# Four attention, scan and convolution layers over eight images: the scans' second product moved from GpSimd to VectorE, key sums taken as four pair sums on TensorE, and three evacuations moved to ScalarE

## The chip, the cores and the metric

The kernel runs on one core of a Trainium2 chip. The core has five engines that run at the same time, each in the order of its own instruction list, and wait for one another by semaphores: TensorE (PE, with its weight loads as PEld), VectorE (DVE), ScalarE (ACT), GpSimd (POOL) and SyncE (SP), which here issues transfers only. The metric is device time in microseconds, from one launch for all eight images. Three runs of the kernel before took 5807.06, 5814.95 and 5815.47 us; their median, 5814.95 us, is the time before.

## The reference

The input is eight images of 256 channels and 32 x 32 pixels, in float32. Four layers follow one another, the first three each as `x + layer(group_norm(x))`:

```python
x = x + _L0_conv_ref(_gn(x), w_qkv, w_out, b_out)   # attention, 8 heads of 64, q and k normalised
x = x + _L1_conv_ref(_gn(x), scaling, quant_w, bias) # 3x3 convolution, 256 -> 256, weights +-1
x = x + _L2_conv_ref(_gn(x), kernel, bias)           # 3x3 convolution, 256 -> 256
x = x + _L3_conv_ref(_gn(x), ...)                    # scans, gates, mixer attention, projections
```

Layer 0 normalises q and k of a head along the 1024 pixels, forms `sim = q k * 10` (1024 x 1024 per head), takes the softmax over the keys and multiplies with v. In layer 3 the 256 channels are cut into four branches of 64. Each branch is widened to 128 channels and passes a selective scan with 16 states per channel, step by step over the 1024 pixels:

```python
h = exp(dt * A) * h + (dt * u) * B     # per channel, state and pixel
y = sum over states of h * C           # + u * D afterwards
```

After the scans come a gate, depthwise convolutions over the pixels, a second attention with 8 heads of 32 (called the mixer here), a Gelu, a depthwise 3x3 convolution and a last projection.

## The kernel before

All work is float32. An image occupies two tiles of 128 channels x 1024 pixels. The stages of an image are recorded as streams, each named by a letter: A (layer 0: q, k, v, attention), O (its output projection), C (the two convolutions), N (norms ahead of the scans), F0 to F3 (what a branch needs before its scan), S (the scans of the four branches), Z0 to Z3 (what follows a branch's scan), B (gates, depthwise convolutions, mixer attention) and E (the end of the image).

**The order is planned on the host.** The engines' methods are wrapped, so that the code records operations instead of issuing them (`Plan`, `Recorded`). `arrange` then lays down an order for all engines together: `gather` joins matmuls into groups, `depend` finds which group needs which and which tiles of rotating pools it uses, `appraise` gives each group a duration from a formula (`cost`, and `STAGGER` for matmuls on parts of the array), and `rank` gives each a due time. The due times come from the table `PACE`: four marks for each stream and image, and a group's due time lies between them by its place in the stream. `arrange` repeatedly takes the engine that can begin earliest and gives it the ready group that can begin soonest, and of equals the one with the earlier due time. A tile of a pool is handed out in the order of due times, and a group that needs a tile waits until one is free. `issue` then emits the instructions in this order, and since every one passes through one helper, all of them carry one line number in the profile, L251. Only the tiles' names tell them apart. The planner's durations decide the order alone, not the time on the chip.

**Attention of layer 0** (`attention`, from L1166, and `pair` in `front_attention`). Two heads make a pair, so an image has four pairs; queries go in two halves of 512 and keys in eight tiles of 128. For each of the 64 steps of an image, two matmuls put scores of 128 keys x 512 queries for both heads into a PSUM tile `big`, ScalarE takes the exponential into a work tile `p` (128 x 1024), and two matmuls multiply `p` with the values into `acc`. VectorE adds the eight `p` of a half into the first of them, with seven `tensor_add` (L1210). After the eighth, `take` sums that tile over its 128 partitions by two matmuls with a matrix of ones, 128 x 64, one per head. The sums go to DRAM, are read back as a 128 x 16 tile `few`, inverted, and spread (`invert`, L1139).

**q, k and v.** `q_and_k` (L1240) copies the projected q and k out of PSUM by VectorE (`a<-big`, shown as `q<-big` and `k<-big`), after which ScalarE squares the PSUM tile for the norms. The four value tiles of an image are copied by VectorE too (L1348). In the mixer, q and k leave PSUM by VectorE with their bias (L1797 to L1802).

**The scans** (`scan_steps`, from L1610). A unit is one branch, one half of the pixels, four states and two of the four groups of 32 channels: 16 units a branch, 64 an image, 512 in all. Its steps are:

```python
pool.tensor_mul(u["hs"], u["du"], both_groups(u["bc"][:, 0]))        # drive: (dt u) B
scalar.activation(u["da"], u["dt"][:, e], AF.Exp, scale=a_neg[...])  # decay, twice, into PSUM
vector.tensor_tensor_scan(hs[:, e], u["da"], hs[:, e], ...)          # scan, twice
pool.tensor_mul(hs, hs, both_groups(u["bc"][:, 1]))                  # weigh: h C
```

In the first half of the pixels, GpSimd also copies the last column of the states (`carry`) for the second half. Every two units, four matmuls with `sel` (128 x 32 each, on the four column parts of the array) add the states into the PSUM tile `y`. The tile `da` has one buffer, `hs` has five. `dt`, `dt u`, B and C of a branch travel through DRAM (`dt_m`, `du_m`, `bc`) to be spread over the partitions; their DRAM pool `dp` has two buffers, and the pool `xdp` that holds the images between C and N has five.

Of the kernel before, what the change touches and what calls it, by code (L numbers as in the profile page):

```python
# [12 lines left out]
F32 = mybir.dt.float32  # L13
# [7 lines left out]
P = 128  # L21
# [13 lines left out]
STAGGER = {(128, 128): 5, (64, 128): 109, (128, 64): 56, (128, 32): 29, (32, 128): 300}  # L35
# [3 lines left out]
        (-805, -722, -708, -698),  # L39
        (-23, 574, 666, 1155),  # L40
        (1968, 2114, 2121, 2171),
        (2852, 2904, 2935, 2987),
        (3583, 3699, 3701, 3730),
        (4216, 4274, 4274, 4274),
        (4659, 4763, 4763, 4927),
        (5576, 5668, 5690, 5902),
    ),
    "B": (
        (2421, 2445, 2644, 2827),
        (3198, 3198, 3283, 3439),  # L50
        (4035, 4035, 4118, 4140),
        (4510, 4598, 4600, 4614),
        (4974, 5354, 5544, 5568),
        (7158, 7158, 7256, 7330),
        (7367, 7615, 7789, 8025),
        (9252, 9434, 9574, 9654),
    ),
    "C": (
        (686, 764, 875, 875),
        (1836, 1987, 2190, 2310),  # L60
        (2369, 2615, 2813, 2937),
        (3296, 3424, 3555, 3745),
        (3992, 4153, 4243, 4479),
        (4472, 4553, 4705, 5147),
        (5548, 5760, 5769, 5918),
        (6309, 6309, 6610, 6714),
    ),
    "E": (
        (2851, 2914, 2949, 3105),
        (3537, 3696, 3801, 3995),  # L70
        (4164, 4309, 4454, 4659),
        (4641, 4925, 5037, 5526),
        (5491, 5660, 5966, 6452),
        (7236, 7974, 8650, 9020),
        (7803, 9469, 9931, 11379),
        (12457, 12492, 12572, 12586),
    ),
    "F0": (
        (291, 291, 349, 383),
        (-602, -270, 49, 2139),  # L80
        (-2209, -2209, -2137, -2137),
        (246, 246, 425, 454),
        (-8960, -8951, -8951, -8832),
        (-1537, -1537, -1537, -1537),
        (-184, -33, 0, 66),
        (4973, 5375, 5378, 5378),
    ),
    "F1": (
        (-437, -436, 487, 491),
        (1752, 1794, 2099, 2171),  # L90
        (49, 129, 515, 3272),
        (3649, 3649, 3706, 3756),
        (4505, 4544, 4594, 4660),
        (2018, 2580, 2690, 2690),
        (5341, 5341, 5353, 5389),
        (4210, 4210, 4210, 4264),
    ),
    "F2": (
        (959, 1013, 1013, 1013),
        (2528, 2641, 2641, 2741),  # L100
        (2573, 3389, 3391, 3447),
        (3918, 4165, 4242, 4261),
        (4191, 4357, 4693, 4693),
        (5559, 5574, 5631, 5782),
        (335, 364, 364, 558),
        (6297, 6519, 6549, 6549),
    ),
    "F3": (
        (1911, 1946, 1948, 1989),
        (2794, 2817, 2817, 2817),  # L110
        (3441, 3441, 3499, 3656),
        (4222, 4328, 4338, 4341),
        (4837, 4862, 4988, 4988),
        (5691, 5860, 5899, 5903),
        (3559, 3559, 3559, 3559),
        (-9601, -9073, -8842, -8730),
    ),
    "N": (
        (-1664, -1664, -1401, -1293),
        (-687, -686, -686, -684),  # L120
        (2795, 3121, 3168, 3219),
        (3804, 3804, 3899, 4110),
        (-242, -22, 1040, 1289),
        (3745, 3749, 3758, 3792),
        (2961, 6267, 6777, 6846),
        (7316, 7506, 7510, 8044),
    ),
    "O": (
        (-582, -391, -354, -341),
        (1469, 1485, 1612, 1612),  # L130
        (2194, 2342, 2343, 2362),
        (3043, 3147, 3181, 3227),
        (3823, 3844, 3951, 4031),
        (4410, 4410, 4410, 4420),
        (5280, 5286, 5297, 5414),
        (6015, 6195, 6218, 6218),
    ),
    "S": (
        (-1634, -1316, -1316, -1316),
        (2298, 2626, 2633, 2722),  # L140
        (3026, 3409, 3755, 3809),
        (3937, 3937, 3937, 3937),
        (516, 2314, 2400, 3371),
        (4794, 4794, 4794, 4846),
        (-550, -490, -490, -490),
        (7436, 7512, 7560, 7593),
    ),
    "V": (
        (463, 463, 764, 872),
    ),  # L150
    "Z0": (
        (-600, -478, -313, -275),
        (-3647, -3176, -3168, -3168),
        (-1138, -1134, -1134, -1132),
        (4211, 4217, 4407, 4407),
        (4725, 4725, 4816, 4915),
        (5804, 5873, 6100, 6457),
        (6544, 6544, 6573, 6597),
        (5426, 5431, 5448, 5490),
    ),  # L160
    "Z1": (
        (-192, 110, 744, 744),
        (2693, 2704, 2773, 2908),
        (2239, 2427, 2448, 2456),
        (4041, 4041, 4551, 4558),
        (4595, 4620, 4620, 4752),
        (5520, 5591, 5873, 5886),
        (1357, 1455, 1455, 1910),
        (2656, 2851, 2916, 3215),
    ),  # L170
    "Z2": (
        (1072, 1232, 1232, 1232),
        (2983, 2983, 2983, 2991),
        (3547, 3551, 3551, 3769),
        (4325, 4372, 4389, 4397),
        (4751, 4773, 4936, 5085),
        (5992, 6074, 6084, 6129),
        (6864, 7140, 7211, 7360),
        (8225, 8272, 8329, 8329),
    ),  # L180
# [2107 lines left out]
```

## Time and profile before

| | |
|---|---|
| Median of three runs | 5814.95 us (5807.06 to 5815.47) |
| Profiled execution | 5817.3 us, span 5815.6 us |
| Mean granted TensorE clock | 0.896 |
| PE busy | 4872.9 us (84%) |
| DVE busy | 3930.9 us (68%) |
| ACT busy | 2709.1 us (47%) |
| POOL busy | 2611.0 us (45%) |
| 512 drives on POOL | 1248.5 us, 2446 ns each |
| 512 weighs on POOL | 1289.2 us, 2519 ns each |
| 448 additions of `p` on DVE | 601.2 us, 1343 ns each |

Times in the profile are microseconds unless marked ns, from one execution. A matmul of 512 float32 columns appears as two records. The chain of waits is followed back from the last instruction, and at each step to what released it; its shares say what set the end. A group's row gives the count, the busy time, the mean of one, and the idle time of its engine just before it with what ended that. A row of a stretch gives the length, then the busy time of PE, PEld, DVE, ACT and POOL with their instruction counts, then the granted TensorE clock as a share of full speed, and the DMA share and rate.

### The profile page before, as it was taken

The page shows a single profiled execution, that of the slowest core. Times are in us where ns is not written, and L with a number is a line of the kernel's source. Part 1 is how long each engine was busy: PE and PEld are TensorE (multiplying, and loading weights), DVE is VectorE, ACT ScalarE, POOL GpSimd, SP SyncE. Part 2 cuts the span into 40 slices and gives each one's busy share as a digit, 9 for nine tenths or more (in the row PEclk, how much of TensorE's full clock was granted, in tenths as well). Part 3 has the DMA queues.
Part 4 walks back from the last instruction along what each step waited for, and adds up shares of the span by engine and source line. Part 5 has one row for each costly group of instructions (what it writes and reads, how often), then busy time and mean ns, then how long its engine had stood idle before and what let it go on. Part 6 is the DMA issues. An engine that isn't in the chain of part 4 may idle for free.

```text
span 5815.6 us, 55053 instructions
## 1 busy us (share of the span) xinstructions
PE 4872.9 (84%) x18086; PEld 1946.9 (33%) x18086; DVE 3930.9 (68%) x5060; ACT 2709.1 (47%) x3353; POOL 2611.0 (45%) x1295
## 2 busy tenths in 40 slices
PE   8998678778998879979899889888899767787695
PEld 3345323322423144332434323332335521221223
DVE  5545787767876667776787657775797775567723
ACT  3333344455453644446354554446453335556342
POOL 0000766287502854046560745518343378287600
PEclk9999889888998889989899989989999877888796
DMA  3123434244413343133522433224333544233301
GB/s 115 42 59 111 120 93 129 73 126 125 110 39 96 104 131 99 53 106 99 145 71 73 138 98 101 82 71 115 99 93 116 146 114 115 62 97 101 88 19 36
DMA packets 262409, 553.34 MB, mean 95 GB/s; under 512 B 65880, under 2 KB 89048, under 8 KB 262112
## 3 DMA queue, kind: packets, MB, share of 16 engines
q1 hardware_dynamic: 178016, 413.36, 25.3%
q10 hardware_dynamic: 84096, 136.35, 8.2%
q8 instruction: 146, 2.39, 0.2%
q14 instruction: 151, 1.24, 0.1%
HBM read 478.72 MB, written 62.39 MB: 93 GB/s over the span
## 4 chain that ended last, share of the span: by engine, by line
PE 49%; DVE 19%; DMA 10%; ACT 8%; POOL 7%; issue 5%; SPq 1%; ACTq 0%; DVEq 0%; POOLq 0%
PE big L251 27%; PE acc L251 9%; PE cv L251 9%; POOL hs L251 7%; DVE hs L251 6%; ACT p L251 3%; DMA dt_m<-dt 2%; ACT da L251 2%; PE y L251 2%; DMA dt<-dt_m 2%; DVE p L251 2%; SPq L251 1%; DVE u L251 1%; DVE room L251 1%; DMA du<-du_m 1%
## 5 line engine op out<-in xcount | busy, mean ns | idle before, releaser
L251 POOL TENSOR_TENSOR hs<-du,bc 128x1024 f32<-128x1024 f32 x512 | 1248.5, 2446 | 2408.6 <-DMA du<-du_m 2157.4
L251 POOL TENSOR_TENSOR hs<-hs,bc 128x1024 f32<-128x1024 f32 x512 | 1289.2, 2519 | 297.7 <-DVE hs L251 251.0
L251 ACT ACTIVATE p<-big 128x1024 f32<-128x1024 f32 x1024 | 1018.4, 1019 | 670.0 <-PE big L251 582.5
L251 ACT ACTIVATE da<-dt,a_neg 128x512 f32<-128x512 f32 x1024 | 707.8, 691 | 1207.1 <-DVE hs L251 956.5
L251 PE MATMUL acc<-p,v 128*64 128x512 f32 x3072 | 854.1, 640 | 141.5 <-ACT p L251 133.3
L251 DVE TENSOR_TENSOR_SCAN hs<-da,carry,hs 128x512 f32<-128x512 f32 x512 | 654.7, 1279 | 333.9 <-ACT da L251 293.8
L251 PE MATMUL cv<-taps,w 128*128 128x256 f32 x3072 | 762.6, 402 | 105.3 <-DVE taps L251 35.4
L251 DVE TENSOR_TENSOR_SCAN hs<-da,hs 128x512 f32<-128x512 f32 x512 | 623.7, 1218 | 330.0 <-ACT da L251 241.5
L251 PEld LDWEIGHTS cv<-taps,w 128*128 128x128 f32 x3072 | 597.7, 200 | 346.8 <-issue 136.6
L251 DVE TENSOR_TENSOR p<-p 128x1024 f32<-128x1024 f32 x448 | 601.2, 1343 | 163.0 <-ACT p L251 125.0
L251 PE MATMUL big<-q,k 64*128 64x512 f32 x2048 | 597.3, 667 | 57.3 <-ACT p L251 33.0
L251 PE MATMUL y<-hs,sel 128*32 128x512 f32 x2048 | 413.3, 689 | 206.4 <-POOL hs L251 199.2
L251 PEld LDWEIGHTS acc<-p,v 128*64 128x64 f32 x3072 | 164.9, 139 | 744.3 <-issue 373.3
L251 PE MATMUL big<-qk,qk 32*128 32x512 f32 x2048 | 369.1, 697 | 46.2 <-ACT raw L251 14.0
L251 PEld LDWEIGHTS big<-q,k 64*128 64x128 f32 x2048 | 164.7, 193 | 448.1 <-issue 236.1
L251 PE MATMUL cv<-p,v 128*64 128x512 f32 x1024 | 288.1, 636 | 2.7 <-DVE xt L251 2.7
L251 PE MATMUL big<-xn,w 128*128 128x512 f32 x512 | 233.5, 606 | 4.3 <-DVE v L251 3.4
L251 PEld LDWEIGHTS y<-hs,sel 128*32 128x32 f32 x2048 | 57.2, 114 | 497.5 <-POOL hs L251 364.7
L251 PEld LDWEIGHTS big<-qk,qk 32*128 32x128 f32 x2048 | 101.9, 198 | 299.8 <-issue 196.4
L251 PE MATMUL big<-o,w 128*128 128x512 f32 x384 | 189.8, 640 | 11.3 <-issue 5.7
L251 POOL COPY carry<-hs 128x2 f32<-128x2 f32 x256 | 107.4, 420 | 169.1 <-DVE hs L251 145.6
L251 DVE SCALAR_TENSOR_TENSOR u<-raw,vec,u 128x1024 f32<-128x1024 f32 x96 | 142.6, 1485 | 37.4 <-ACT u L251 36.4
(228 smaller groups left out, 5448.8 us busy)
## 6 DMA issues: line engine op xcount, KB each, us to landing
bc<-bc SPq DMA_DIRECT2D x1024, 128.0 KB
w<-wc ACTq DMA_DIRECT2D x384, 256.0 KB
dt<-dt_m SPq DMA_DIRECT2D x512, 128.0 KB
du<-du_m SPq DMA_DIRECT2D x512, 128.0 KB
rs<-inv SPq DMA_DIRECT2D x64, 256.0 KB
dt_m<-dt SPq DMA_DIRECT2D x64, 256.0 KB
du_m<-a SPq DMA_DIRECT2D x64, 256.0 KB
w<-in_wqk ACTq DMA_DIRECT2D x64, 128.0 KB
```

What stands on the lines that cost most here:

```text
L251: made = op["call"](*args, **kwargs).ins
```

## The change

- The weigh is a product on VectorE, and the carry copy is one on ScalarE.
- VectorE adds each second `p` to the one before it. This leaves four sums of two per half instead of one sum of eight. `take` sums all four over the partitions: eight matmuls with ones of 128 x 32, even pair sums into rows 0 and 32 and odd ones into rows 64 and 96, which leaves two partial sums for each head. One transfer carries the four rows to DRAM instead of two; `invert` reads two `few` and adds them on VectorE.
- The copies of q, k and v in layer 0, and q and k of the mixer with their bias, are ScalarE's. (The value tile of the mixer stays with VectorE.)
- In the planner: a fill (a transfer from DRAM or a memset into a pool tile) is due no earlier than its first use; a matmul group also claims the tile `v` or `x` that its evacuation will write; the assumed extra time of matmuls on 32 rows is 90 instead of 300; every mark in `PACE` is new. In the kernel before, the marks of S begin at -1634, 2298, 3026, 3937, 516, ...; in the new table they begin at 496, 980, 1470, 1967, 2458, 2907, 3371, 3655.
- `dp` has four buffers and `xdp` eight.

```diff
-STAGGER = {(128, 128): 5, (64, 128): 109, (128, 64): 56, (128, 32): 29, (32, 128): 300}
+STAGGER = {(128, 128): 5, (64, 128): 109, (128, 64): 56, (128, 32): 29, (32, 128): 90}
+CLAIMED = (("vp", "v"), ("xp", "x"))
...
+    users = defaultdict(list)
+    for n, op in enumerate(ops):
+        for a in op["ins"]:
+            if in_psum(a):
+                users[a.tensor.name].append(groups[of[n]])
+    for g in groups:
+        if g.engine == 0:
+            out = ops[g.ops[0]]["outs"][0].tensor.name
+            for u in users[out]:
+                for t in u.tiles:
+                    if rooms[t][0] in CLAIMED and t not in g.tiles:
+                        g.tiles.append(t)
...
+    first_use = [None] * len(groups)
+    for n in reversed(range(len(groups))):
+        if groups[n].fetches and first_use[n] is not None:
+            due[n] = max(due[n], first_use[n])
+        for k in groups[n].after:
+            first_use[k] = due[n] if first_use[k] is None else min(due[n], first_use[k])
...
-    dp = plan.pool("dp", 2, space=DRAM)
+    dp = plan.pool("dp", 4, space=DRAM)
...
-    xdp = plan.pool("xdp", 5, space=DRAM)
+    xdp = plan.pool("xdp", 8, space=DRAM)
...
-            if add_up:
-                if kt == 0:
-                    pair["sum"] = u["p"]
-                else:
-                    vector.tensor_add(pair["sum"], pair["sum"], u["p"])
+            if kt == 0:
+                pair["sums"] = []
+            if kt % 2 == 0:
+                pair["sums"].append(u["p"])
+            else:
+                total = pair["sums"][-1]
+                vector.tensor_add(total, total, u["p"])
...
-                vector.tensor_copy(a, ps)
+                scalar.copy(a, ps)
                 scalar.activation(ps, ps, AF.Square, accum_out=ss[:, i : i + 1])
...
+                for n, total in enumerate(totals):
+                    for e in range(2):
+                        at = (2 * (n % 2) + e) * 32
+                        tensor.matmul(
+                            ps[at : at + 32, 0:HALF],
+                            ones,
+                            total[:, HALVES[e]],
+                            start=n < 2,
+                            stop=n >= len(totals) - 2,
+                        )
...
-            vector.tensor_copy(
-                v[:, kt : kt + 2].rearrange("p a b -> p (a b)"), ps
-            )
+            scalar.copy(v[:, kt : kt + 2].rearrange("p a b -> p (a b)"), ps)
...
-                pool.tensor_copy(carry[:, u["q"], g : g + 2], hs[:, :, HALF - 1])
-            pool.tensor_mul(hs, hs, both_groups(u["bc"][:, 1]))
+                scalar.copy(carry[:, u["q"], g : g + 2], hs[:, :, HALF - 1])
+            vector.tensor_mul(hs, hs, both_groups(u["bc"][:, 1]))
...
-                    vector.tensor_scalar(
-                        q, ps, col("ain_b", t), 32.0**-0.5, ALU.add, ALU.mult
+                    scalar.activation(
+                        q, ps, AF.Identity, bias=q_b[:, t : t + 1], scale=32.0**-0.5
                     )
...
-                    vector.tensor_scalar_add(k, ps, col("ain_b", at))
+                    scalar.activation(k, ps, AF.Identity, bias=col("ain_b", at))
```

## The prediction

> **What bounds the kernel now.** I read the page's busy shares first, then the chain of waits, then the scan's groups, then the stretches between the first and last state sum of each image.
>
> ```profile
> PE 4872.9 (84%) x18086; PEld 1946.9 (33%) x18086; DVE 3930.9 (68%) x5060; ACT 2709.1 (47%) x3353; POOL 2611.0 (45%) x1295
> ...
> PE 49%; DVE 19%; DMA 10%; ACT 8%; POOL 7%; issue 5%; SPq 1%; ACTq 0%; DVEq 0%; POOLq 0%
> PE big L251 27%; PE acc L251 9%; PE cv L251 9%; POOL hs L251 7%; DVE hs L251 6%; ACT p L251 3%; DMA dt_m<-dt 2%; ACT da L251 2%; PE y L251 2%; DMA dt<-dt_m 2%; DVE p L251 2%; SPq L251 1%; DVE u L251 1%; DVE room L251 1%; DMA du<-du_m 1%
> ```
>
> TensorE is the fullest engine, yet only half of the chain is its own. The other half is latency, largely of the scans: POOL `hs`, DVE `hs`, ACT `da`, and the transfers of `dt` and `du`.
>
> ```profile
> 625.00:1062.00 437.00, 330.92 (x1149) 117.37 (x1148) 353.15 (x356) 195.35 (x259) 317.04 (x150) 0.86 0.40 111
> 1184.00:1596.00 412.00, 346.72 (x1402) 137.35 (x1398) 310.44 (x321) 210.31 (x280) 305.27 (x152) 0.89 0.44 122
> 3917.00:4460.00 543.00, 486.29 (x1961) 184.44 (x1960) 400.13 (x500) 290.82 (x373) 309.85 (x152) 0.96 0.39 107
> 4614.00:4975.00 361.00, 243.68 (x888) 82.66 (x878) 240.91 (x207) 157.60 (x204) 295.68 (x147) 0.78 0.42 115
> 5097.00:5488.00 391.00, 292.19 (x1088) 93.30 (x1084) 293.58 (x272) 196.41 (x241) 315.73 (x153) 0.82 0.37 105
> ```
>
> These rows are the scans of images 0, 1, 5, 6 and 7. POOL has the same 300 us or so of work in each: 57% of image 5's stretch, but 73% to 82% of the others. There POOL sets the pace, and TensorE works at low density (busy time times granted clock, over the length): 0.65, 0.75, 0.86, 0.53 and 0.61. Over the whole span, fine stretches added up the same way give 4432 us of full-clock work, a density of 0.76.
>
> ```profile
> L251 POOL TENSOR_TENSOR hs<-du,bc 128x1024 f32<-128x1024 f32 x512 | 1248.5, 2446 | 2408.6 <-DMA du<-du_m 2157.4
> L251 POOL TENSOR_TENSOR hs<-hs,bc 128x1024 f32<-128x1024 f32 x512 | 1289.2, 2519 | 297.7 <-DVE hs L251 251.0
> ...
> L251 DVE TENSOR_TENSOR p<-p 128x1024 f32<-128x1024 f32 x448 | 601.2, 1343 | 163.0 <-ACT p L251 125.0
> ```
>
> ```profile
> 2617.80 1.28 DVE L251 TENSOR_TENSOR_SCAN hs<-da,carry,hs 128x512 f32<-128x512 f32 x1 [0.76 <-ACT da L251]
> ...
> 2619.12 0.69 ACT L251 ACTIVATE da<-dt,a_neg 128x512 f32<-128x512 f32 x1
> ...
> 2619.91 1.28 DVE L251 TENSOR_TENSOR_SCAN hs<-da,carry,hs 128x512 f32<-128x512 f32 x1 [0.83 <-ACT da L251]
> ...
> 2621.96 1.28 DVE L251 TENSOR_TENSOR_SCAN hs<-da,carry,hs 128x512 f32<-128x512 f32 x1 [0.76 <-ACT da L251]
> ```
>
> With one `da` buffer, decay and scan alternate: scans start 2.1 us apart, 4.2 us a unit. POOL needs 2.45 + 2.52 us and, in half of the units, a 0.42 us carry copy: 5.2 us a unit. So in a dense scan POOL comes last, by 1.0 us.
>
> **The change, part by part.** I sum on the chain of the profiled execution (5817.3 us, span 5815.6 with 1.7 around it); it lies 2.3 us above the median.
>
> *Weigh.* 512 products of 2519 ns leave POOL (-1289 us), with 256 carry copies (-107), and POOL falls from 45% to about 21%. On DVE the same form, `p<-p`, has a median of 1225 ns and a mean of 1343. POOL `hs` is 6.5% of the chain, 378 us; drive and weigh have equal counts and nearly equal durations, so 189 each. The weighs' share shrinks by (2.52-1.34)/2.52: **-88**.
>
> *Drive.* It no longer stands behind a weigh in POOL's list and can run ahead as far as five `hs` buffers allow. Of its 189 us, one drive of 2.45 us in each of 64 branch halves stays at most exposed when POOL restarts (157); at best all but the 32 branch starts go (78 stay). Between -32 and -111, I take **-75**, nearer the best, since POOL will be idle ahead of most.
>
> *Additions of p.* 192 of 448 go: DVE -258 us. DVE `p` is 2% of the chain, 96 us in full; 3/7 of it: **-41**.
>
> *Pair sums.* The nearest rows:
>
> ```profile
> 1747.27 1.03 PE L251 MATMUL big<-p,ones 128*64 128x512 f32 x4
> 1748.23 0.38 PE L251 MATMUL big<-mean_w,room 128*128 128x1 f32 x2
> ...
> 2618.88 1.06 PE L251 MATMUL y<-hs,sel 128*32 128x512 f32 x8
> ...
> 2619.87 1.08 PE L251 MATMUL acc<-p,v 128*64 128x512 f32 x4
> ```
>
> Two column tiles with ones occupy TensorE 0.96 us until the next matmul; four tiles (`y`) 0.99, entry from another tiling and return included. Two groups of four cost 1.98 against 0.96: 64 x 1.02 = **+65**, all counted, since TensorE is the fullest engine. The Trainium skill, "TensorEngine Tiling (Array Packing)", section Key Properties, says that a change of tiling mode drains TensorE; sums of 128x32 among products of 128x64 add two such changes per half, where the old sums needed none. A full drain would mean one un-overlapped 0.69 us record each, 64 x 2 x 0.69 = 88 us more. The trace shows at most 0.06 us above the 0.93 us pitch of unswitched `acc` groups, so I keep the row.
>
> *VectorE's load.* +512 x 1.225 = +627; port waits as below, +60; additions -258; 96 copies at 1215 ns -117; 32 of `qk` at 1271 ns -41; 32 small additions of `few` at some 0.2 us, +6: net +277, to 72% of the old span. If all fits into its waits for `da` (535 us in total) it costs 0, if none does, 277. DVE is 19% of the chain, so **+53**. The new `few` addition also waits for two transfers where one was waited for; what is queued behind is whatever VectorE does next, scans included. The old wait was 79.7 us in 17 times; it is the reciprocal's, moved ahead by one instruction, and I count nothing more.
>
> *ScalarE's load.* 96 copies at about 1011 ns (`raw<-big`), 32 with bias at about 1110 (`gate`), 256 carries at about 0.22 (POOL takes 0.19 undisturbed; between 0.19 and 0.42): +97+36+56 = +189 us on an engine at 47%. Copy and square now follow one another on ScalarE, which removes its 82 us wait for VectorE's copy of q. ACT is 8% of the chain: +15 against some -15; **0**. Without that cover: +189.
>
> *Transfers.* SP issues 128 fewer row stores, 64 more wide ones, 32 more `few` reads: 32 fewer at about 0.34 us, **0**.
>
> *Order.* Fills, claims, buffers and due times cost no instructions, but move all of them. The listing of both orders gives the number of other matmuls between an image's first and last `y`: before 446, 573, 779, 738, 718, 853, 317, 416; after 760, 816, 770, 874, 982, 752, 469, 396. Between the scans of neighbouring images, 150, 431, 207, 319, 223, 244, 160 become 22, 209, 227, 71, 141, 193, 110. The scans thus lie nearly end to end, and the thin ones (0, 1, 6) get more TensorE work beside them. `dt` and `du` through DRAM take about 396 us of the chain, 12 us for each of 32 branches. If half of the eight image starts are hidden that gives -50; none and a new misfit of equal size +50; all of 16 branches -200. I take **-50**.
>
> Sum: -88-75-41+65+53-50 = -136, so 5817-136 = 5681, or 5679 against the median. One check: 4432+65 us of TensorE work in 5679 is a density of 0.79; the scans of images 3 to 5 reach 0.79 to 0.86 today, and what the new order puts beside the scans resembles those. The check would allow 0.80 (5620), so I lean to it by a third: **5660**.
>
> **The port.** The rule that speaks against the change: the Trainium skill, "SBUF — State Buffer", section "SBUF: two separate sides", says VectorE with two SBUF inputs and GpSimd share a port pair under an exclusive lock, and the loser waits for the whole instruction. The trace shows such waits:
>
> ```profile
> L251 DVE TENSOR_TENSOR p<-p x448: 1169/1225/3395, 55.7 to 4440.5; 128x1024 f32<-128x1024 f32 x150
> 4697.64 3.35 DVE L251 SCALAR_TENSOR_TENSOR fd<-r,vec,fd 128x1024 f32<-128x1024 f32 x1
> ```
>
> A maximum of 3395 is 1225 plus most of a drive. But the mean is only 0.12 us above the median, although POOL was over 70% busy in dense scans: the order avoids most meetings. By the row, 512 x 0.12 = 60 us, in the sum. By the rule with meetings at random, a drive holds the port 2.36 of 4.7 us a unit, and half of the products wait 1.18 us: 302 us. Drive and weigh stood in one list and could never meet; now they can. I take the row.
>
> **Rivals.**
> *The port decides (slower).* Place: the weigh in dense scans, with the next scan behind it. At the random price, 242 us more than in the sum, all on the path: 5660+242 = 5900. It decides once the products' mean passes about 1.64 us (155 us of gain over 512, on top of 1.34). Against it: the 0.12 us of the row, and less POOL work to meet. 9%.
> *VectorE becomes the bound.* All 277 us instead of 53 on the path: 5660+224 = 5884 at worst; with half, 5770. For it: DVE reached 81% in the first row above. Against: scans wait for `da` 535 us, room that others can fill. Near 5770: 15%.
> *The order does more than counted.* TensorE's density reaches 0.82: 4497/0.82 = 5485. For it, the clock: 0.96 where PE is 90% busy, 0.78 where 67%; less idle time also means a faster clock. The sum leaves that out. 18%.
> *It doesn't show.* POOL's relief lies beside TensorE-bound work, and pair sums eat the rest: 5815. 5%.
>
> **How the numbers follow.** Forecast 53%, spread 5580 to 5740. A measurement can tell about 0.2% (12 us) from no change. Faster: 53+18 and 15 near 5770, 0.86; same 0.05; slower 0.09. The range leaves a tenth below and a tenth above: 5500 to 5810; the likeliest case's own is 5580 to 5740.
>
> **What would show it.** POOL near 1230 us; DVE near 4200; the weigh's mean on DVE below 1.45 us (above 1.64 the port decides); pair sums near 2 us a half; the waits of `y` for POOL `hs` (199 us) gone and not replaced by as much for DVE `hs`; clock above 0.90; scans of images 0, 1 and 6 at density above 0.75. DVE above 80% with TensorE's density unchanged would make me wrong.

## The result and the profile after

The changed kernel took 5719.57 us (median of four runs, 5714.33 to 5720.27), the kernel before 5815.21 us in the same comparison (four runs, 5807.06 to 5819.97). The ratio is 0.9835, with a 95% interval from 0.9818 to 0.9852: 96 us less, where the forecast had 155 less. The sign held, and the wait that was to shrink did shrink, in six of the eight images. The size came out as 0.6 of the forecast, and the experiments suggest that this is a sum of larger errors of both signs.

Of the changed kernel's page, the busy times and the chain of waits:

```profile
PE 4851.9 (85%) x18854; PEld 1945.2 (34%) x18854; DVE 4044.5 (71%) x5285; ACT 2843.0 (50%) x3737; POOL 1309.9 (23%) x527
...
PE 52%; DVE 22%; issue 9%; ACT 8%; DMA 7%; SPq 1%; POOL 1%; ACTq 0%; DVEq 0%; POOLq 0%
PE big L252 29%; PE cv L252 10%; PE acc L252 10%; DVE hs L252 10%; ACT p L252 3%; PE y L252 2%; DVE room L252 2%; ACT da L252 2%; DVE u L252 2%; DMA dt_m<-dt 1%; DMA du_m<-a 1%; DMA dt<-dt_m 1%; DVE fd L252 1%; SPq L252 1%; DMA bc<-bc 1%
```

GpSimd's share of the chain fell from 7% to 1%, that of transfers from 10% to 7%; VectorE's `hs` rose from 6% to 10%. VectorE is busy for 114 us more than before, not for the 277 that I had added up.

The groups that changed:

```profile
L252 DVE TENSOR_TENSOR hs<-hs,bc 128x1024 f32<-128x1024 f32 x512 | 725.9, 1421 | 64.3 <-ACT carry L252 59.4 <-DMA bc<-bc 0.6 <-DMA du<-du_m 0.3
L252 DVE TENSOR_TENSOR p<-p 128x1024 f32<-128x1024 f32 x256 | 331.3, 1296 | 325.4 <-ACT p L252 194.1 <-PE acc L252 130.8
L252 PE MATMUL big<-p,ones 128*32 128x512 f32 x1024 | 126.1, 599 | 4.1 <-ACT p L252 4.1
L252 POOL TENSOR_TENSOR hs<-du,bc 128x1024 f32<-128x1024 f32 x512 | 1307.0, 2570 | 4069.7 <-PE y L252 1880.9 <-DMA du<-du_m 1722.3 <-DMA bc<-bc 170.1
```

The weigh's mean is 1421 ns, below the 1.64 us at which the port would have decided. The pair sums take 126.1/64 = 1.97 us a half. Ahead of the drives GpSimd idles for 4070 us; 1881 of these end when `y` gives a state buffer back, 1722 when `du` arrives. Where `y` ends the wait, the drives have run ahead as far as the buffers go.

The stretches from the first to the last `y` of images 0, 1, 5, 6 and 7 (length; busy time and count of PE, PEld, DVE, ACT, POOL; granted clock; DMA share and rate):

```profile
688.00:1225.00 537.00, 460.79 (x1777) 191.16 (x1776) 411.06 (x543) 267.34 (x379) 151.83 (x62) 0.90 0.39 113
1240.00:1760.00 520.00, 468.17 (x1888) 177.89 (x1888) 412.80 (x516) 292.57 (x396) 154.43 (x59) 0.93 0.38 106
3835.00:4316.00 481.00, 432.92 (x1764) 144.31 (x1756) 386.23 (x402) 271.94 (x368) 152.42 (x59) 0.95 0.39 105
4438.00:4868.00 430.00, 300.43 (x1194) 113.23 (x1190) 366.06 (x358) 202.40 (x285) 151.31 (x59) 0.79 0.39 110
4989.00:5409.00 420.00, 291.33 (x1049) 90.50 (x1048) 364.76 (x328) 210.73 (x281) 156.50 (x59) 0.78 0.33 96
```

TensorE's density (busy time times clock, over the length) is 0.77, 0.84, 0.86, 0.55 and 0.54, where it was 0.65, 0.75, 0.86, 0.53 and 0.61. Images 0 and 1 gained as forecast, 6 hardly, and 7 lost; in these last two VectorE is busy for 85% and 87%.

So the time is best cut in four: up to the first `y`, images 0 to 5, the last two images, and the tail. The second and third of these in the kernel before:

```profile
625.00:4460.00 3835.00, 3304.13 (x12402) 1300.85 (x12402) 2775.58 (x3459) 1885.65 (x2357) 1943.55 (x950) 0.91 0.36 100
4460.00:5488.00 1028.00, 770.41 (x2782) 302.36 (x2782) 700.15 (x766) 477.76 (x588) 645.71 (x320) 0.82 0.38 107
```

and in the changed kernel:

```profile
688.00:4316.00 3628.00, 3225.70 (x12775) 1265.65 (x12774) 2787.38 (x3526) 1944.99 (x2597) 964.38 (x379) 0.93 0.37 104
4316.00:5409.00 1093.00, 770.19 (x2846) 308.65 (x2844) 892.11 (x960) 516.39 (x680) 331.05 (x128) 0.79 0.34 99
```

| stretch | before | after | difference |
|---|---|---|---|
| to the first `y` | 625 | 688 | +63 |
| images 0 to 5 | 3835 | 3628 | -207 |
| last two images | 1028 | 1093 | +65 |
| tail, to the span's end | 328 | 309 | -19 |

The first row is work laid ahead of the scans, no loss by itself: start to last `y` of image 5 is -144. The third row is a loss. The same shows in the wait of the state sums, first in the kernel before, images 0 to 5 and then the last two (busy, mean ns, then idle time just before, with what ended it):

```profile
L251 PE MATMUL y<-hs,sel 128*32 128x512 f32 x1536 | 291.5, 670 | 118.7 <-POOL hs L251 116.9 <-DVE u L251 1.6
L251 PE MATMUL y<-hs,sel 128*32 128x512 f32 x512 | 121.8, 745 | 87.7 <-POOL hs L251 82.3 <-DVE u L251 5.4
```

then in the changed kernel:

```profile
L252 PE MATMUL y<-hs,sel 128*32 128x512 f32 x1536 | 242.3, 633 | 32.6 <-DVE hs L252 30.8 <-DVE u L252 1.7
L252 PE MATMUL y<-hs,sel 128*32 128x512 f32 x514 | 130.9, 765 | 157.4 <-DVE hs L252 157.4
```

In six images the wait of `y` for the weigh fell from 117 to 31 us. In the last two it rose from 82 to 157. Over the whole execution it is 188 us where it was 199, and the two halves hide each other in that total.

### The profile page after: what moved, and what is told of

It reads as the page before. It is cut to its first block, busy times and chain, and to the rows that moved or that the text cites. A ratio compares the mean times of both kernels' runs of the same rounds, so it can differ in the third digit from the quotient of the medians.

```text
span 5717.7 us, 56860 instructions
## 1 busy us (share of the span) xinstructions
PE 4851.9 (85%) x18854; PEld 1945.2 (34%) x18854; DVE 4044.5 (71%) x5285; ACT 2843.0 (50%) x3737; POOL 1309.9 (23%) x527
## 4 chain that ended last, share of the span: by engine, by line
PE 52%; DVE 22%; issue 9%; ACT 8%; DMA 7%; SPq 1%; POOL 1%; ACTq 0%; DVEq 0%; POOLq 0%
PE big L252 29%; PE cv L252 10%; PE acc L252 10%; DVE hs L252 10%; ACT p L252 3%; PE y L252 2%; DVE room L252 2%; ACT da L252 2%; DVE u L252 2%; DMA dt_m<-dt 1%; DMA du_m<-a 1%; DMA dt<-dt_m 1%; DVE fd L252 1%; SPq L252 1%; DMA bc<-bc 1%
## 5 line engine op out<-in xcount | busy, mean ns | idle before, releaser
L252 POOL TENSOR_TENSOR hs<-du,bc 128x1024 f32<-128x1024 f32 x512 | 1307.0, 2570 | 4069.7 <-PE y L252 1880.9
L252 PE MATMUL cv<-taps,w 128*128 128x256 f32 x3072 | 780.9, 405 | 90.2 <-DVE xt L252 30.4
L252 DVE TENSOR_TENSOR hs<-hs,bc 128x1024 f32<-128x1024 f32 x512 | 725.9, 1421 | 64.3 <-ACT carry L252 59.4
L252 DVE TENSOR_TENSOR p<-p 128x1024 f32<-128x1024 f32 x256 | 331.3, 1296 | 325.4 <-ACT p L252 194.1
L252 PE MATMUL y<-hs,sel 128*32 128x512 f32 x2048 | 372.6, 666 | 189.9 <-DVE hs L252 188.1
L252 PE MATMUL big<-qk,qk 32*128 32x512 f32 x2048 | 339.5, 691 | 36.7 <-DVE z L252 9.1
L252 DVE SCALAR_TENSOR_TENSOR room<-room,vec,room 128x992 f32<-128x992 f32 (+1 forms) x128 | 165.5, 1293 | 12.7 <-ACT room L252 11.3
L252 PE MATMUL big<-fd,w 128*128 128x512 f32 x256 | 135.3, 681 | 43.6 <-DVE fd L252 31.9
```

Source lines behind the costliest of these rows:

```text
L252: made = op["call"](*args, **kwargs).ins
```

## The experiments

My theory: the gain is GpSimd's relief in images 0 to 5, and the shortfall is VectorE, in the last two images now busier than TensorE (82% against 70%). The rivals: the order alone made the gain; the weigh alone would have made it; the port ate it. Where I give a difference to the changed kernel, it is the difference of the two ratios times 5815 us, and its uncertainty is the root of the sum of the squares of both half intervals.

### One part at a time, with the order laid anew

The first four runs change a part and let the planner lay a new order for it.

The weigh and the carry alone, in the kernel before:

```diff
-                pool.tensor_copy(carry[:, u["q"], g : g + 2], hs[:, :, HALF - 1])
-            pool.tensor_mul(hs, hs, both_groups(u["bc"][:, 1]))
+                scalar.copy(carry[:, u["q"], g : g + 2], hs[:, :, HALF - 1])
+            vector.tensor_mul(hs, hs, both_groups(u["bc"][:, 1]))
```

> The kernel before with the weigh on VectorE and the carry copy on ScalarE, and nothing else; the host's planner lays the order anew with the old due times. If the move of the weigh by itself is the gain: 5700 to 5760 us. If it needs the room that pair sums and ScalarE copies make on VectorE (415 us less there) and the new due times: VectorE busy near 4490 us (3931 + 560) and a time of 5815 or above. If the order is what gains: 5800 to 5850.

Measured: 6307.9 us, ratio 1.0849 (1.0830 to 1.0867).

The reverse, the weigh and the carry back on GpSimd in the changed kernel (the diff above, turned round):

> The changed kernel with weigh and carry copy back on GpSimd, order laid anew with the new due times. If the weigh's move is needed for the gain: 5800 us or more, POOL above 70% busy in most scans. If the new due times and claims make the gain: within 25 us of the changed kernel (5695 to 5745). If VectorE bounds the last two images, their stretch from the last y of image 5 to the last y of image 7 becomes shorter than the changed kernel's 1093 us, near the old 1028, even if the whole is slower.

Measured: 6248.5 us, ratio 1.0755 (1.0737 to 1.0773).

The operations of the kernel before with the new planner (first use, claims, 90 for 300), the new due times and pools (the diff in outline):

```diff
-PACE = {...}          # marks of the kernel before
+PACE = {...}          # marks of the changed kernel
...
-    dp = plan.pool("dp", 2, space=DRAM)
+    dp = plan.pool("dp", 4, space=DRAM)
-    xdp = plan.pool("xdp", 5, space=DRAM)
+    xdp = plan.pool("xdp", 8, space=DRAM)
```

> The kernel before, every operation on its old engine, with the changed planner: new due times, claims, fills due with first use, larger DRAM pools. If the order is the cause of the gain: 5720 to 5760 us. If the order only pays with the shorter scans: 5800 us or slower.

Measured: 6214.7 us, ratio 1.0697 (1.0669 to 1.0725).

In the changed kernel, half of the weighs of the last two images on GpSimd:

```diff
-            vector.tensor_mul(hs, hs, both_groups(u["bc"][:, 1]))
+            late = plan.stream[1] >= 6 and u["gp"] == 1
+            (pool if late else vector).tensor_mul(hs, hs, both_groups(u["bc"][:, 1]))
```

> The changed kernel, but in images 6 and 7 every second weigh goes back to GpSimd (group pair 1), order laid anew. If VectorE (90% busy there) bounds these two images: 32 products fewer per image, 39 us of VectorE work each, so the stretch from the last y of image 5 to that of image 7 falls from 1093 us by 40 to 90 and the time to 5640 to 5690. If their bound is the recurrence of decay and scan, or the thin TensorE work: no change, 5705 to 5735. If GpSimd's products collide with VectorE's on the shared port: slower than 5735.

Measured: 5789.4 us, ratio 0.9967 (0.9952 to 0.9982).

By their ratios all four are slower than the changed kernel, by 77 to 590 us. Moving the weigh to VectorE costs 8.5% of the time before in the one kernel, and moving it back costs 9.2% in the other, which cannot both be the price of the weigh. Such a pattern says more of the orders than of the parts. So I tried what a new order costs when no work moves at all, with one constant of the planner changed:

```diff
-STAGGER = {..., (32, 128): 90}
+STAGGER = {..., (32, 128): 120}
```

> The changed kernel's work without any change, its order laid anew because one of the planner's tie-breaking constants is another (120 for 90). If an order that the due times were not fitted to costs by itself what the re-laid kernels so far lost, 5780 to 6200; if orders of the same work scatter little, 5700 to 5740, and what those kernels lost was due to their moved work.

Measured: 5917.3 us, ratio 1.0177 (1.0148 to 1.0207). The same instructions in another order cost 3.42% of 5815 us, 199 +- 20 us: more than twice the whole gain. Its stretches for images 0 to 5, the last two, and the tail:

```profile
688.00:4378.00 3690.00, 3233.78 (x12638) 1265.28 (x12631) 2810.94 (x3522) 1930.30 (x2577) 967.39 (x379) 0.92 0.35 102
4378.00:5566.00 1188.00, 816.37 (x2938) 312.96 (x2934) 868.28 (x919) 524.08 (x693) 336.55 (x128) 0.78 0.31 92
5566.00:5918.00 352.00, 241.12 (x922) 102.15 (x918) 113.78 (x187) 120.05 (x119) 0.00 (x0) 0.80 0.08 25
```

That is 62, 95 and 44 us longer than in the changed kernel. The marks fit one set of operations and one set of the planner's durations. The first four runs therefore decide nothing about the parts; they only refute that the new marks help whatever work they are given.

### The same order, another engine

From here on the planner sees the changed kernel's operations and lays the changed kernel's order (in one run, the kernel before's), and only when an instruction is issued does it go to another engine. All other instructions keep their sequence on every engine. The helper:

```diff
+    def instead(call, on, *args, **kwargs):
+        if plan.recording:
+            plan.ops[-1].update(call=call, on=on, args=(args, kwargs))
```

**The weigh on GpSimd** (the carry stays on ScalarE):

```diff
             vector.tensor_mul(hs, hs, both_groups(u["bc"][:, 1]))
+            instead(nc.gpsimd.tensor_mul, 3, hs, hs, both_groups(u["bc"][:, 1]))
```

> The changed kernel with every instruction in its place in each queue, the second product alone issued on GpSimd in place of VectorE: 512 products, so VectorE is lighter by 512 x 1.42 = 727 us and GpSimd heavier by 512 x about 2.35 = 1203 us. If the gain is GpSimd's relief, GpSimd is again what the scans are laid against (2 x 2.35 us for each pass of eight states where VectorE took about 5.5), and the time goes to the kernel before or over it, 5815 to 6050. If the new order alone made the gain, 5720 to 5740. If VectorE's load is what holds the changed kernel back, below 5700.

Measured: 5793.3 us, ratio 0.9969 (0.9961 to 0.9976), so the weigh's engine is worth 78 +- 11 us in this order. The time is 22 us below the range for GpSimd's relief and 53 above the range for the order alone. Images 0 to 5 and the last two:

```profile
688.00:4408.00 3720.00, 3256.66 (x12776) 1267.74 (x12774) 2599.32 (x3151) 1943.88 (x2598) 1896.76 (x758) 0.92 0.36 102
4408.00:5488.00 1080.00, 772.98 (x2844) 311.45 (x2844) 768.07 (x832) 515.72 (x680) 625.14 (x256) 0.79 0.34 100
```

Against this run the changed kernel saves 92 us in images 0 to 5 and loses 13 in the last two. That refutes both halves of my theory's simple form. The weigh's engine accounts for under half of the 207 us in images 0 to 5, and the last two images are 52 us longer than before (1080 against 1028) even with the weigh on GpSimd and VectorE at 71%. The state sums of these two wait for 143 us, nearly as long as in the changed kernel (157), where they had waited for 82 before:

```profile
L252 PE MATMUL y<-hs,sel 128*32 128x512 f32 x512 | 132.1, 745 | 143.1 <-POOL hs L252 143.0
```

No addition of `p`, no pair sum and no copy of layer 0 falls into this stretch, so in this order most of the loss does not come from these parts or from the weigh's engine. Beside eight copies of the mixer, what is left is the order with its pools, and one thing more: the carry stays on ScalarE here, and GpSimd's weighs idle for 492 us in all, 75 of them in the last two images, until a carry is done. No run took both back in this order, so a part of the 78 and of the 52 us may be the price of that detour.

**Half of the weighs of the last two images on GpSimd**, now in the same order:

```diff
             vector.tensor_mul(hs, hs, both_groups(u["bc"][:, 1]))
+            if plan.stream[1] >= 6 and u["gp"] == 1:
+                instead(nc.gpsimd.tensor_mul, 3, hs, hs, both_groups(u["bc"][:, 1]))
```

> The changed kernel with every instruction in its place in each queue, and in images 6 and 7 every second second product (64 of them) issued on GpSimd. VectorE loses 64 x 1.42 = 91 us of work in the 850 us of those two scans where it is 90 per cent busy, GpSimd, 23 per cent busy, takes on 64 x 2.4 = 154 us. If VectorE is the bound of the last two images, these get shorter by 30 to 80 us: 5640 to 5690. If the two engines' meeting on memory or the length of the chain drive, scan, second product, y sets the pace there, 5710 to 5760.

Measured: 5696.9 us (5689.2 to 5706.7), ratio 0.9806 (0.9778 to 0.9835). The stretch that the edit touches:

```profile
4308.00:5380.00 1072.00, 756.53 (x2846) 302.25 (x2844) 832.51 (x896) 516.01 (x680) 476.00 (x192) 0.80 0.34 101
```

It is 21 us shorter than in the changed kernel, for 60 us less VectorE work. Against the changed kernel the ratios differ by 17 +- 19 us, not resolved by itself. But no run of the one overlaps a run of the other, and most of the gain lies where the edit is (images 0 to 5, which it doesn't touch, are 10 us shorter in this execution). The result falls between the two expectations: VectorE's load seems to be part of the loss in the last two, and at 1072 us the greater part of it remains. The same edit with the order laid anew had cost 77 us. (Over the scans of these two images in the changed kernel VectorE is 86% busy, not 90% as the expectations say.)

**More sharing**: also a quarter of the weighs of images 0 to 5 (`u["gp"] == 1` and `u["h"] == 1`).

> The changed kernel with every instruction in its place in each queue, the second products shared: half of those of images 6 and 7 on GpSimd as in the run of the late share, and of images 0 to 5 a quarter (96). Against the run of the late share VectorE has 96 x 1.42 = 136 us less and GpSimd 96 x 2.5 = 240 us more in the scans of images 0 to 5. If moving the product pays in proportion there (the full move was worth 92 us in these images), a quarter moved back costs 23: 5720. If VectorE at 0.82 to 0.87 already holds these scans back: 5650 to 5690.

Measured: 5704.2 us, ratio 0.9803 (0.9784 to 0.9823): 19 +- 15 us less than the changed kernel, and no difference from the late share alone that can be told. Images 0 to 5 in the late share, then here:

```profile
690.00:4308.00 3618.00, 3215.64 (x12776) 1260.84 (x12775) 2782.49 (x3526) 1944.61 (x2597) 973.57 (x379) 0.93 0.36 105
```

```profile
689.00:4332.00 3643.00, 3226.72 (x12773) 1262.64 (x12774) 2744.68 (x3430) 1945.32 (x2597) 1206.12 (x475) 0.93 0.36 104
```

The 25 us between them are near the first expectation, but they compare a short execution of the one (5690.7 us) with the longest of the other (5720.0), and the medians differ by 7 us. The second expectation, a gain, is refuted. Taking a quarter of the weighs off VectorE brings nothing in these images; whether VectorE's load from them costs nothing, or GpSimd takes back what it saves, the run doesn't say.

**The weigh on VectorE in the order of the kernel before:**

```diff
             pool.tensor_mul(hs, hs, both_groups(u["bc"][:, 1]))
+            instead(nc.vector.tensor_mul, 1, hs, hs, both_groups(u["bc"][:, 1]))
```

> The kernel before with every instruction in its place in each queue, the second product alone issued on VectorE: GpSimd lighter by about 1203 us, VectorE heavier by 727. If the product's move is the gain by itself and the order counts for little, 5700 to 5780. If the gain needs an order laid for it, 5800 to 5950, because the old order has VectorE's other work between the scans spaced for GpSimd's pace.

Measured: 6085.2 us, ratio 1.0476 (1.0447 to 1.0504), beyond either expectation. The move that gains 78 us in the new order costs 277 in the old one. Image 0's scan there, then the last two images:

```profile
633.00:1105.00 472.00, 330.64 (x1144) 119.53 (x1140) 409.94 (x419) 194.55 (x258) 174.72 (x88) 0.84 0.36 102
...
4662.00:5754.00 1092.00, 792.27 (x2784) 310.02 (x2782) 843.64 (x895) 479.42 (x588) 360.89 (x192) 0.80 0.35 101
```

In image 0 VectorE is at 87%, where it was at 81% and the stretch at 437 us. It still has the 192 additions and 128 copies that the whole change takes away. So the weigh alone makes no gain. In the last two images its move alone costs 64 us here (1092 against 1028), as much as the whole change does. The carry stays on GpSimd in this run, and GpSimd idles for 621 us ahead of it until a scan is done. VectorE's scans, however, wait for the drives for 72 us, where they waited for 121 before, so the loss does not show there.

**The copies of q, k and v back on VectorE**, in the changed order:

```diff
                 scalar.copy(a, ps)
+                instead(nc.vector.tensor_copy, 1, a, ps)
...
             scalar.copy(v[:, kt : kt + 2].rearrange("p a b -> p (a b)"), ps)
+            instead(nc.vector.tensor_copy, 1, v[:, kt : kt + 2].rearrange("p a b -> p (a b)"), ps)
...
                     scalar.activation(k, ps, AF.Identity, bias=col("ain_b", at))
+                    instead(nc.vector.tensor_scalar_add, 1, k, ps, col("ain_b", at))
```

> The changed kernel with every instruction in its place in each queue, but the copies of q, k and v of layer 0 (96) and q and k of the mixer (32) issued on VectorE again, as before the change. VectorE gets 96 x 1.215 + 32 x 1.27 = 157 us more, ScalarE 96 x 1.01 + 32 x 1.11 = 133 us less. By the forecast's terms (ScalarE 0, VectorE's load 53/277 of what is added) 5750. If neither engine's load of this size counts: 5710 to 5730. If ScalarE's load was the cost: below 5700. If nearly all of it lies on the path: 5850.

Measured: 5765.4 us, ratio 0.9913 (0.9893 to 0.9932): 45 +- 15 us more, for 157 us of VectorE work. ScalarE had 120 us less to do here. The run gives only the net of the two, so that ScalarE's copies cost nothing fits it but is not shown by it.

**Three of four pair additions done twice**, which gives VectorE back as many additions as the change removed:

```diff
                 vector.tensor_add(total, total, u["p"])
+                if kt > 1 and plan.recording:
+                    plan.ops[-1]["times"] = 2
```

> The changed kernel with every instruction in its place in each queue, but three of the four pair additions of a half done twice in a row on VectorE: 192 additions more, as many as the change removed, 192 x 1.29 = 248 us. (It changes what is computed: the second of these pairs counts twice in the sums of keys.) By the forecast's terms (removed additions -41, and their part of VectorE's load -258 x 53/277 = -49) 5810. If VectorE has slack where attention runs: 5720 to 5750. If it all lies on the path: 5965.

Measured: 5883.7 us, ratio 1.0115 (1.0095 to 1.0136): 163 +- 15 us more, 1.8 times the 90 of the forecast's terms. Images 0 to 5 and the last two:

```profile
695.00:4482.00 3787.00, 3276.80 (x12772) 1275.79 (x12766) 3031.44 (x3670) 1944.50 (x2597) 974.03 (x379) 0.92 0.35 100
4482.00:5573.00 1091.00, 776.14 (x2848) 310.53 (x2844) 886.78 (x961) 516.38 (x680) 332.58 (x128) 0.79 0.34 99
```

159 us of it lie in images 0 to 5, where VectorE rises from 77% to 80% only. In the waits of ScalarE (total, count, longest) one grows from 5.2 us to 75.7, the exponential waiting for an addition to free its tile:

```profile
ACT da L254 <- DVE hs L254: 869.3, 433, 12.4
...
ACT p L254 <- DVE p L254: 75.7, 33, 7.6
```

And scans behind an addition are later: ScalarE's wait for `hs` was shorter in the changed kernel:

```profile
ACT da L252 <- DVE hs L252: 814.8, 421, 12.3
```

An addition stands in VectorE's list between what attention and what the scans wait for.

**Half of the pair sums' matmuls left out:**

```diff
+                        if plan.recording:
+                            if n >= 2:
+                                plan.ops[-1]["times"] = 0
+                            else:
+                                plan.ops[-1]["args"][1]["stop"] = True
```

> The changed kernel with every instruction in its place in each queue, but the second half of the pair sums' matmuls left out: four for each half in place of eight, so that TensorE has 64 x about 1.0 us = 63 us less, as much as the pair sums added to it. (It leaves out half of each sum of keys.) If these matmuls cost the end their whole length, as the forecast counted: 5655. If TensorE's idle time absorbs them: 5700 to 5720.

Measured: 5709.6 us, ratio 0.9812 (0.9792 to 0.9832), 13 +- 15 us less. TensorE has 58 us less of these:

```profile
L254 PE MATMUL big<-p,ones 128*32 128x512 f32 x512 | 68.1, 604 | 2.0 <-ACT p L254 2.0
```

The stretch up to the first `y`:

```profile
0.00:679.00 679.00, 612.80 (x2242) 274.95 (x2246) 275.32 (x657) 271.68 (x351) 14.53 (x20) 0.96 0.28 86
```

With no scan beside the attention, 9 us go (688 to 679). The matmuls left out there would have taken 15 us, half of the 31.0 us of the 256 matmuls with ones in this stretch. From image 0 on nothing is gained (3627 us against 3628, then 1099 against 1093).

## Why the prediction was right and wrong

**The sign was right, by its steps.** GpSimd's part of the chain went, the drives run ahead, VectorE did not become the bound of the whole, and the port did not decide. What the steps were worth, each from a run that undoes it, or nearly so, in the order of the changed kernel, stands beside the forecast's terms. These are given with their part of VectorE's load (53 us over 277, 0.19 a microsecond):

| step | forecast | measured |
|---|---|---|
| weigh and drive: -88 - 75 + 0.19 x 687 | -32 | -78 +- 11 |
| additions: -41 - 0.19 x 258 | -90 | -163 +- 15 |
| copies: -0.19 x 158, ScalarE 0 | -30 | -45 +- 15 |
| pair sums | +65 | +13 +- 15 |
| order (forecast), what is left over (measured) | -50 | +177 +- 36 |

The last entry is -96 less the four above it. It supposes that the four add up, which no run shows: each was undone in an order laid for the whole, so each also pays for the misfit that it causes. I read it only as a sign. The forecast's column adds up to some -136; the further -19 that made 155 came from leaning to the check by density, not from a step.

**The step that does not stand is "Order", as a term with a gain of its own.** I took -50 us for it, half of the image starts' transfers hidden, with counts of matmuls in support. The transfers did shrink on the chain: the pieces of `dt` and `du` add up to 354 us before and to 221 after, without the queue's own time. (Pieces called "issue", 187 us in all, may hide some of the rest; see below.) But the order is no part with a gain of its own: with the old operations the new planner, marks and pools cost 405 us (ratio 1.0697), and without any moved work one other constant costs 199. What the weigh's move is worth hangs on the order too: in the one it gains 78 us, in the other it loses 277.

**Where the missing 59 us may lie.** The last two images lost 65 us, which no term of mine had. Without that loss the gain would have been near the forecast, but the forecast had no terms by stretch, so this match of sizes is no proof. In the new order 13 of the 65 us go with the weigh's engine and 52 stay when it is moved back. In the old order the weigh's move alone costs 64 there. Order and VectorE's load can thus each make this loss, and they do not add. That the order does it through the place of other VectorE work is what the trace suggests. The taps of the last depthwise convolution there, before:

```profile
L251 DVE SCALAR_TENSOR_TENSOR room<-room,vec,room 128x961 f32<-128x961 f32 (+1 forms) x16 | 22.0, 1375 | 1.0 <-ACT room L251 0.8
```

and in the changed kernel:

```profile
L252 DVE SCALAR_TENSOR_TENSOR room<-room,vec,room 128x961 f32<-128x961 f32 (+1 forms) x44 | 60.5, 1374 | 0.2
```

28 more of them, 38 us, stand among these scans, 16 taken from earlier images and 12 from the tail. A piece of image 6's scan, in order of time (start, length, engine, operation, idle time before it):

```profile
4561.49 1.21 DVE L252 TENSOR_TENSOR_SCAN hs<-da,hs 128x512 f32<-128x512 f32 x1
...
4562.62 1.22 DVE L252 SCALAR_TENSOR_TENSOR room<-room,vec,room 128x992 f32<-128x992 f32 x1
4562.79 0.19 ACT L252 COPY carry<-hs 128x2 f32<-128x2 f32 x1 [2.05 <-DVE hs L252]
...
4563.77 1.28 DVE L252 TENSOR_SCALAR a<-big,vec 128x1024 f32<-128x1024 f32 x1
4564.96 1.21 DVE L252 SCALAR_TENSOR_TENSOR room<-room,vec,room 128x961 f32<-128x961 f32 x1
...
4566.09 1.22 DVE L252 TENSOR_TENSOR_SCAN hs<-da,hs 128x512 f32<-128x512 f32 x1
...
4568.06 1.22 DVE L252 TENSOR_TENSOR_SCAN hs<-da,hs 128x512 f32<-128x512 f32 x1 [0.76 <-ACT da L252]
...
4570.26 1.22 DVE L252 TENSOR_TENSOR_SCAN hs<-da,hs 128x512 f32<-128x512 f32 x1 [0.97 <-ACT da L252]
4571.40 1.23 DVE L252 SCALAR_TENSOR_TENSOR room<-room,vec,room 128x992 f32<-128x992 f32 x1
...
4572.54 0.69 DVE L252 TENSOR_SCALAR dt<-raw 128x1024 f32<-128x1024 f32 x1
4573.14 1.21 DVE L252 SCALAR_TENSOR_TENSOR room<-room,vec,room 128x961 f32<-128x961 f32 x1
4574.27 1.22 DVE L252 SCALAR_TENSOR_TENSOR raw<-dt,raw 128x1024 f32<-128x1024 f32 x1
...
4575.48 1.22 DVE L252 TENSOR_TENSOR hs<-hs,bc 128x1024 f32<-128x1024 f32 x1
...
4576.76 1.92 PE L252 MATMUL y<-hs,sel 128*32 128x512 f32 x4 [8.67 <-DVE hs L252]
```

The first scan shown is the last of its unit, since a carry follows it at once. In this half of the pixels each unit has one carry and one weigh, both in the same sequence, so the weigh at 4575.5 is this unit's. It comes 12.8 us after the scan's end. Between them VectorE does four taps, three operations of a branch, a tiny one (not shown) and three scans of later units, and it idles for 1.7 us only; TensorE has idled for 8.67 us when the `y` follows. No run moved the taps, so their part is argued, not shown.

**VectorE's load was priced too low, and its size too high.** The price of 0.19 us for each microsecond came from the chain's share. The additions cost 163/(192 x 1.31) = 0.65, the copies 45/157 = 0.29, the late weighs 21/60 = 0.35. The share of an engine in the chain says where the path runs, not what more work on it would cost. The rival in which VectorE becomes the bound was therefore half right: not for the whole span, but for the additions beside scans and for the last two images. The size came out at +114 us of busy time instead of +277, for the most part because VectorE's other instructions became shorter (last section).

**The pair sums were priced too high.** Their length was right, 1.97 us a half. That all of it counts, "since TensorE is the fullest engine", was not: the 13 us cannot be told from zero, and none of it shows where scans run beside the attention. (The prediction also took 0.93 us as the pitch of unswitched `acc` groups. Three groups in a row, from 1744.65 to 1747.27 in the kernel before, have 0.87, so four tiles with their two switches cost up to 0.12 us more, not 0.06.)

**The markers.** POOL 1310 us against 1230, since the drive's mean rose from 2446 to 2570 ns; DVE 4044 against 4200; clock 0.898, just short of the 0.90 named. Images 0 and 1 passed a density of 0.75, image 6 did not. The wait of `y` was said not to be replaced by as much, and was replaced nearly in full, 157 of the 188 us in the last two images. There the named sign of being wrong also came, VectorE above 80% (85% and 87%) with TensorE's density not better (0.55 and 0.54, before 0.53 and 0.61).

**What stays open:** how much of the 207 us in images 0 to 5 belongs to the order alone, and which of its parts (marks, fills, claims, pools) matters, since no run takes them apart. Also 187 us of the chain's "issue" share lie in four pieces ahead of GpSimd's drives, from 818, 886, 3214 and 3315 us on, which I cannot read.

## What to carry to other kernels

When the order of a kernel is fitted to its work, judge one part by swapping its engine inside the finished order, and read the answer as the part's worth in that order; laying the order anew for each variant measures the misfit instead. Work added to an engine at 77%, in order between two other engines' waits, cost two thirds of its length here, so read the price from what stands behind each instruction, not from the engine's share of the chain. And cut a wait by stretches before calling it unchanged: here 86 us gained in six images and 75 lost in two left 11 to see.

The fastest kernels measured that leave nothing out are the changed one with half of the last two images' weighs on GpSimd in the same order, 0.9806 (0.9778 to 0.9835) of the kernel before, and the one with more sharing, 0.9803 (0.9784 to 0.9823). They cannot be told apart.

## What the runs showed of the hardware

Taking an operation off GpSimd made VectorE's other instructions shorter. Their durations added up, without weighs, additions of `p`, additions of `few` and the moved copies, are 3358 us before and 3207 after; with the weigh back on GpSimd in the new order they are 3488, and with it on VectorE in the old order 3219. With the weigh back on GpSimd in the new order the additions' mean is 1544 ns, not 1296, and VectorE is busy for only 313 us less although 726 us of weighs left it. So over half of what the move costs VectorE comes back as shorter waits. My forecast had counted only the weigh's own waits: 512 x 0.12 = 60 us by the row and 302 by chance meetings, against 512 x (1.421 - 1.224) = 101 us measured.

Even the smallest operations wait. The shortest, median and longest durations of two groups (tile by tile, with the first and last start) in the run with the weigh on GpSimd:

```profile
L252 DVE SCALAR_TENSOR_TENSOR norm<-t,y x24: 140/160/2270, 30.7 to 4662.3; 128x2 f32<-128x2 f32 x24
...
L252 DVE TENSOR_TENSOR_SCAN hs<-da,hs x512: 1153/1223/1225, 658.6 to 5426.6; 128x512 f32<-128x512 f32 x171
```

An operation on two columns can take 2270 ns, nearly a whole product of GpSimd (a median of 2357), while 512 scans, which read `da` out of PSUM, never wait. Both agree with the Trainium skill, "SBUF — State Buffer", section "SBUF: two separate sides", by which only a VectorE operation with both inputs in SBUF (or in a mode that uses both port pairs) contends with GpSimd, and then for the whole instruction.
